# Two-layer image block: first strip's projection moved into the second unit of an image change, the mean of the second normalization later, the kept strip normalized after the copies of the weighted values

## The chip, the cores and the metric

The kernel runs on one core of one Trainium2 chip. The metric is the device time of one execution in microseconds. 3 runs of the kernel before took 3533.04 to 3534.71 us, with a median of 3534.49 us.

## The reference

The input x has 8 images of 384 channels and 64 x 64 pixels, all in float32. Two layers are added to it:

- Layer 1: group normalization (32 groups), then, per pixel, a layer normalization over the channels and a product with a 384 x 1152 matrix for queries, keys and values. Half of the channels go to attention in 8 x 8 windows (branch 0, 4 heads), the other half to attention in windows shifted by 4 pixels with wrap-around (branch 1, 4 heads, with a mask). Both have a position bias and a softmax. The joined result goes through the 384 x 384 output projection and is added to x.
- Layer 2: group normalization of the sum, a 384 x 384 product per pixel, in each 8 x 8 patch a Fourier transform, a filter and the transform back, a 3 x 3 depthwise convolution, a gelu of one half times the other half, and a 192 x 384 product, added to x.

```
x = x + attention(_gn(x))          # layer 1
x = x + fourier_conv(_gn(x))       # layer 2
```

The second group normalization needs mean and variance over the whole image. So layer 2 of an image cannot begin before layer 1 of that image has been projected for all of its strips.

## The kernel before, in words

**Strips and units.** An image is cut into 8 strips of 8 rows, 512 pixels each (NS = 8), with the channels in three groups (KC = 3) on 128 partitions. A strip's attention takes two units, one for each branch: strip s of image b has its units at 16 b + 2 s and one more. Layer 2 of image b runs through the same units as layer 1 of image b + 1: strip s starts at unit 16 b + 18 + 2 s. Units are counted from 0 in the text. An even unit holds four `mix` products (pt) and the end of an older strip (`finish`, pw), an odd one the transform back (`back`, pz) and usually a projection (pr). The image change of image b is units 16 b + 16 and 16 b + 17: both of the last projections of image b lie at it, those of strip 7 and of strip 0. Strip 0 comes so late because its first rows, by the wrap-around, come from strip 7's shifted windows. Its data lies in a buffer of its own (tag `ow`, one buffer). Unit 16 b + 17 has no projection in the kernel before and is the shortest.

**Order.** Every piece of work is put down with a place by `at(place, piece, ...)`. The list is sorted by place and issued in this order. Matmuls stay exactly in this order (`keep_in_program_order`). On the other engines, a scheduler takes, when an engine is free in its own account of time, the ready instruction that was issued first; the order is then fixed. Extra edges without a wait fix an order on one engine: `after_softmax` (behind the last softmax instruction issued) and `after_out` (behind the last copy of the weighted values, `zs["out"]`). Large transfers on SP wait for a gate, the last copy of the first qk tile (`in_dense_work`).

**Pieces that matter here**, for a unit w:

- `scores` (w + 0.05): 64 small matmuls into pS. `weights`, `exponent`, `divide` (0.12 to 0.26): softmax on DVE and ACT.
- `turn` (w + 0.80): transposes the weights into pT; ACT copies them to eT. `apply` (w + 1.00): 64 small matmuls of eT with v into pA. `put` (w + 1.07): ACT copies pA to o (L602 to L605 for branch 1), and ten or five transfers on POOL's queue write o to the projection's input oT.
- pS, pT, pA and one half of pw share two PSUM pairs (`psum2`); all other products share four PSUM banks (`psum`).
- `qk_tile`, `v_tile` (places 0.14 to 0.88 of the unit before): products pq and pvv with their copies on ACT.
- `project`: 9 matmuls pr of 512 columns for a strip, in three groups m, each followed on DVE by an addition into x_add. `keep`: bn_stats of the three parts. `store`: x_add to memory.
- `second_mean`: bn_aggr (mv_b), matmul pm, four small DVE instructions. `second_std`: matmul pv, square root on ACT (sd, with a table load), reciprocal and shift on DVE.
- `normal_x1`: three activations xn for a strip of layer 2. Strip 0's x_add stays in its buffer and is used again here (the load "mix" for s = 0 is only a renaming); the other strips come from memory (x_mix). xn has one buffer.
- `conv`: 24 multiply-adds ("taps", zz L785) a strip on DVE, most of DVE's work.

**Empty instructions.** `EMPTY` gives, unit by unit, a number of empty TensorE instructions that are issued among the dense matmuls of that unit (qk tiles and projections).

Of the kernel before, what the change touches and what calls it, by code (L numbers as in the profile page):

```python
# [8 lines left out]
AF = mybir.ActivationFunctionType  # L9
# [9 lines left out]
NS = SW // WS  # L19
# [6 lines left out]
C_ID, C_ONES, C_GRP, C_FWD, C_INV, C_MASK = 0, 128, 256, 384, 512, 640  # L26
C_PICK = C_MASK + 3 * 64
N_CONST = C_PICK + 2
EMPTY = (129, 0, 0, 96, 52, 0, 0, 98, 11, 124, 11, 124, 3, 124, 11, 124, 11, 45, 43, 124, 52, 123, 11, 124,
         11, 124, 11, 124, 3, 124, 11, 124, 11, 45, 43, 124, 52, 123, 11, 124, 11, 124, 11, 124, 3, 124, 11, 124,  # L30
         11, 45, 43, 124, 52, 123, 11, 124, 11, 124, 11, 124, 3, 124, 11, 124, 11, 45, 43, 124, 52, 123, 11, 124,
         11, 124, 11, 124, 3, 124, 11, 124, 11, 45, 43, 124, 52, 123, 11, 124, 11, 124, 11, 124, 3, 124, 11, 124,
         11, 45, 43, 124, 52, 123, 11, 124, 11, 124, 11, 124, 11, 0, 0, 115)

STATS_AT = 2.16, 4.16, 5.16, 6.16, 7.16, 8.16, 9.16, 10.16

# [2 lines left out]
def block_kernel(ctx: ExitStack, tc: tile.TileContext, out, x, consts, fsel, wqk, wv, bqk, bv,  # L39
                 wp, bp, lng, lnb, rpb1, rpb2, w_in, w_dw, w_out, filt):  # L40
    nc = tc.nc
    B = x.shape[0]
# [72 lines left out]
    for s in range(NS):  # L115
        tag, bufs = ("x", 5) if s < 5 else (("xn", 1), ("ow", 1), ("y2", 1))[s - 5]
        t = strip(tag, bufs, f"x_first{s}")
# [28 lines left out]
    for j, to, n, t, hp, of in blocks:  # L146
        nc.gpsimd.dma_start(out=bqk_sb[to:to + n].rearrange("p (b j) -> p b j", b=2)[:, :, j],
                            in_=bqk[of:of + n, 4 * t:4 * t + 4].rearrange("p (b i) -> p b i", b=2)[:, :, hp])
# [19 lines left out]
    for br, tab in ((0, rpb1), (1, rpb2)):  # L168
        raw = sb.tile([P, 2, 64], F32, tag="t2", bufs=3, name=f"rpb_raw{br}")
        raw_bias.append(raw)  # L170
        for h in range(4):
            half = slice(h % 2 * 64, h % 2 * 64 + 64)
            for y2 in range(WS):
                nc.gpsimd.dma_start(
                    out=raw[half, h // 2, y2 * WS:(y2 + 1) * WS],
                    in_=bass.AP(tab.tensor, h * 225 + y2 * 15, [[15, 8], [1, 8], [1, 8]]),
# [109 lines left out]
    def image_order(t):  # L286

        return t.rearrange("p (r w c) -> p w r c", r=WS, w=NS)

    def by_window(t):  # L290

        return t.rearrange("p (w r c) -> p w r c", w=NS, r=WS)
# [7 lines left out]
    def at(place, piece, *args):  # L300
        plan.append((place, len(plan), piece, args))

    xs, ys, y2s, qks, vs, os_, ots, x1s, zs = ({} for _ in range(9))
# [10 lines left out]
    gs0, gs1, st0s, st1s, x1d = ({} for _ in range(5))  # L314
# [9 lines left out]
    def in_dense_work(i):  # L324


        if zs.get("gate"):
            behind(i, zs["gate"], mybir.DependencyClass.Sync, "transfer in dense work")
# [4 lines left out]
    def load(b, s, what):  # L333

        if b == 0 and (what == "stats" or what == "norm" and s < 3):
            xs[b, s, what] = first_x[s]
            return
        if what == "mix" and s == 0:
            xs[b, s, what] = xs.pop((b, s, "add"))
            return  # L340
        t = xs[b, s, what] = strip("x", 5, f"x_{what}_{b}_{s}")
        src = x1d[b][s] if what in ("mix", "finish") else rows_of(x[b], s)
        in_dense_work(nc.sync.dma_start(out=t, in_=src))
# [239 lines left out]
    def after_out(i):  # L583
        if "out" in zs:
            behind(i, zs["out"], mybir.DependencyClass.NoSync, "weighted values first")
# [47 lines left out]
        strip_stats(st1s[b], s, xs[b, s, "add"])  # L633

    def store(b, s):
        in_dense_work(nc.sync.dma_start(out=x1d[b][s], in_=xs[b, s, "add"] if s == 0 else xs.pop((b, s, "add"))))


    def second_mean(b):
# [9 lines left out]
    def normal_x1(b, s):  # L649

        t, (gain, shift) = xs.pop((b, s, "mix")), gs1[b]
        xn = x1s[b, s] = strip("xn", 1, f"xn_{b}_{s}")
        for k in range(KC):
            nc.scalar.activation(by_window(xn[:, k, :]), image_order(t[:, k, :]), AF.Identity,  # L654
                                 bias=shift, scale=gain)

    def mix(b, s, i):

# [189 lines left out]
    for b in range(B):  # L848
        first = 2 * NS * b

        for s in range(NS):
            u = first - 16 + STATS_AT[s] if b else -10 + 0.1 * s
            at(u, load, b, s, "stats")
            at(u + (0.5 if b else 0.05), input_stats, b, s)
        if b == 0:

            at(-9.99, pack_qk, 0)
            at(-9.98, qk_weights, 0)
            at(-9.97, v_weights)
            at(-9.96, pack_qk, 1)  # L860
            at(-9.95, qk_weights, 1)
            for place, key in ((-9.82, ("qk", 0)), (-9.62, ("v",)), (-2.9, ("qk", 1))):
                at(place, take_off, *key)
            at(-2.64, qk_bias, 0)
            at(-2.58, v_bias)
            at(-2.58, qk_bias, 1)
            at(-2.7, spread_first)
            at(-0.6, position_bias, 0)
            at(-0.4, position_bias, 1)
            at(0.2, out_bias)  # L870
            at(0.2, filter_weights)
        at(first - 4.8 if b else -8, input_mean, b)
        at(first - 4.4 if b else -7.9, input_std, b)
        for s in range(NS):
            u = first + 2 * s

            v = u - 4
            early = 1.75 if b == 0 and s == 1 else 0
            at(v - 0.84 - early, load, b, s, "norm")
            at(v + 0.15 - early, group_normal, b, s)  # L880
            at(v + 0.45 - (1.35 if early else 0), ln_square, b, s)
            if b:
                at(v + 0.985, small_tiles, v + 1)
            at(v + 0.99 if (b, s) != (0, 1) else -2.69, ln_sums, b, s)
            at(v + 0.99 if (b, s) != (0, 1) else -2.6, ln_row, b, s)
            at(v + 1.35, ln_scale, b, s)

            if s:
                at(v + 1.50, shifted_half, b, s - 1, 1)
            else:  # L890
                at(u - 1.15, shifted_half, b, NS - 1, 1)
            at(u - 1.2 if s < NS - 1 else v + 1.55, shifted_half, b, s, 0)
            for br in range(2):
                w = u + br
                for t in range(3):
                    at(w - 1 + (0.14, 0.34, 0.55)[t], qk_tile, b, s, br, t)
                for g in range(2):
                    at(w - 1 + ((0.78, 0.86), (0.67, 0.88))[br][g], v_tile, b, s, br, g)
                at(w + 0.05, scores, b, s, br)
                at(w + 0.12, weights, b, s, br)  # L900

                at(w + 0.13, exponent, b, s, br)
                at(w + (0.23, 0.26)[br], divide, b, s, br)
                at(w + 0.80, turn, b, s, br)
                at(w + 1.00, apply, b, s, br)
                at(w + 1.07, put, b, s, br)

            if 0 < s < NS - 1:
                places = [u + 3 + f for f in (0.27, 0.45, 0.70)]
            else:  # L910
                places = [first + 2 * NS + f + (0.0 if s else 0.24) for f in (0.36, 0.44, 0.52)]
            at(int(places[0]) - 0.84, load, b, s, "add")
            for m in range(KC):
                at(places[m], project, b, s, m)
            at(places[2] + 0.1, keep, b, s)
            at(int(places[2]) + 1.15, store, b, s)
        first += 2 * NS
        at(first + 1.25, second_mean, b)
        at(first + (1.90 if b < B - 1 else 1.995), second_std, b)
        if b == B - 1:  # L920
            at(first + 2, tap_matrices)
        for s in range(NS):
            u = first + 2 + 2 * s
            at(u - 0.84, load, b, s, "mix")
            at(u + 0.02, normal_x1, b, s)
            for i in range(4):
                at(u + (0.28, 0.45, 0.60, 0.78)[i], mix, b, s, i)
            for j in range(2):
                at(u + (0.995, 1.02)[j], transform, b, s, j)
            if b < B - 1:  # L930
                at(u + 1.985, small_tiles, u + 2)
            at(u + 1.99, back, b, s)
            at(u + 2.08 if b < B - 1 or s < NS - 1 else u + 1.991, borders, b, s)

            for n, m in enumerate((0, 2, 1)):
                for tap in range(1, 6):
                    at(u + (2.62, 3.10, 3.5)[n] + 0.05 * tap + (0.4 if n == 2 and tap > 3 else 0), conv, b, s, m, tap)
                for tap in range(6, 9):
                    at(u + 4.2 + 0.25 * (n * 3 + tap - 6) / 9, conv, b, s, m, tap)
            if (b, s) in on_pool:  # L940
                for place, taps in ((2.45, (0, 1)), (2.8, (2, 3)), (3.15, (4, 5)), (4.15, (6, 7)), (4.3, (8,))):
                    at(u + place, pool_taps, b, s, taps)
            if (b, s) in on_pe:
                at(u + 2.3, conv_taps, b, s)
            at(u + 5.16, load, b, s, "finish")
            at(u + 4.5, gate, b, s)
            at(u + 6.10, finish, b, s)
# [5 lines left out]
    order = [p[2:] for p in sorted(plan, key=lambda p: p[:2])]  # L953
    dense, empty, counts = [], [0] * len(order), list(EMPTY)
    for i, (piece, args) in enumerate(order):
# [116 lines left out]
```

## Time and profile before

| | us |
|---|---|
| median of 3 runs | 3534.49 |
| profiled execution, device time | 3528.99 |
| its span, first to last instruction | 3526.8 |
| steady odd unit / even unit | 24.26 / 28.25 |
| units 48, 49, 50, 51, 52 (third image change) | 43.7, 18.15, 29.39, 17.69, 28.66 |

| engine | busy us | share |
|---|---|---|
| PE (TensorE matmuls) | 3450.3 | 98% |
| DVE | 3062.2 | 87% |
| ACT | 2535.8 | 72% |
| POOL | 1055.3 | 30% |

All times of instructions and units come from the one profiled execution. The mean granted TensorE clock is 0.992. In lines of the profile, `out<-in` are the program's names of tiles, Lnnn is a line of the kernel, and a bracket at the end of a timeline row is the idle time of the engine before the row and what ended it ("issue": nothing that the profile shows). Nearly all matmuls have line L62, that of a helper, so they are told apart by their tiles.

### The profile page before, as it was taken

The numbers are of one execution on the slowest core, as the hardware profiler recorded it, in microseconds if no ns is written. First come the engines' busy times: TensorE is split into PE (matmuls) and PEld (weight loads), VectorE is DVE, ScalarE is ACT, GpSimd is POOL, SyncE is SP. The second block draws the span as 40 slices with busy tenths as digits, with TensorE's granted clock in tenths as the row PEclk, the third lists the DMA queues.
The fourth block names the chain that finished last, engine by engine and source line by source line (L and its number), as shares of the span: only waits on it lengthen the run. The fifth ranks groups of instructions, "written<-read, shape, count | busy, mean of one in ns | idle before, by whom it ended". The sixth has DMA issues, their size and how long they took to land.

```text
span 3526.8 us, 93350 instructions
## 1 busy us (share of the span) xinstructions
PE 3450.3 (98%) x36454; PEld 2192.9 (62%) x36454; DVE 3062.2 (87%) x4330; ACT 2535.8 (72%) x4069; POOL 1055.3 (30%) x1688
## 2 busy tenths in 40 slices
PE   7999999999999999999999999999999999999888
PEld 5666666666666666666666666666666666666554
DVE  5676589889998899998999889998899988987987
ACT  5877777768777687776777767777777767776574
POOL 6433222323222232222233223232232223222244
PEclk8999999999999999999999999999999999999999
DMA  4343234323343334333344324433234333323432
GB/s 135 117 128 100 88 119 138 107 101 133 130 148 108 117 107 153 120 121 109 119 136 140 119 89 141 138 116 133 101 118 156 113 107 109 108 99 104 160 109 81
DMA packets 176101, 421.13 MB, mean 119 GB/s; under 512 B 26656, under 2 KB 29243, under 8 KB 175688
## 3 DMA queue, kind: packets, MB, share of 16 engines
q1 hardware_dynamic: 138832, 364.25, 29.6%
q0 software_dynamic: 36416, 50.65, 5.1%
q8 instruction: 316, 5.18, 0.6%
q14 instruction: 97, 0.79, 0.1%
q10 hardware_dynamic: 440, 0.27, 0.0%
HBM read 263.92 MB, written 100.79 MB: 103 GB/s over the span
## 4 chain that ended last, share of the span: by engine, by line
PE 87%; DVE 8%; ACT 2%; issue 1%; DMA 1%; POOL 0%; SPq 0%; ACTq 0%; POOLq 0%; DVEq 0%
PE pq L62 26%; PE pr L62 14%; PE pvv L62 13%; PE pt L62 11%; PE pw L62 6%; PE pA L62 3%; PE pz L62 3%; PE pT L70 3%; PE pS L62 3%; DVE zz L785 2%; PE pf L62 2%; DVE acc L785 1%; PE ln L62 1%; DVE t L681 1%; ACT tap L753 1%
## 5 line engine op out<-in xcount | busy, mean ns | idle before, releaser
L785 DVE SCALAR_TENSOR_TENSOR zz<-z,dw_sb,zz 128x512 f32<-128x512 f32 x1331 | 1026.5, 797 | 10.8
L62 PE MATMUL pq<-y,wqk_sb 128*128 128x512 f32 x2160 | 989.4, 597 | 0.9 <-ACT kcd L470 0.7
L615 POOL DMA_DIRECT2D oT<-o x960 | 480.2, 508 | 963.4 <-ACT z L718 431.2
L62 PEld LDWEIGHTS pq<-y,wqk_sb 128*128 128x128 f32 x2160 | 403.1, 190 | 448.0 <-issue 407.3
L62 PE MATMUL pt<-wi_sb,xn 128*128 128x384 f32 x1536 | 535.1, 487 | 3.0 <-ACT xn L654 3.0
L62 PE MATMUL pr<-oT,wp_sb 128*128 128x512 f32 x1152 | 523.9, 593 | 1.6 <-DMA oT<-o 1.6
L62 PE MATMUL pvv<-wv_sb,y 128*128 128x192 f32 x2880 | 507.4, 326 | 0.0
L62 PEld LDWEIGHTS pvv<-wv_sb,y 128*128 128x128 f32 x2880 | 471.7, 190 | 48.6 <-issue 33.7
L62 PEld LDWEIGHTS pt<-wi_sb,xn 128*128 128x128 f32 x1536 | 290.9, 191 | 232.8 <-issue 74.1
L452 POOL COPY y<-y 128x384 f32<-128x384 f32 x112 | 86.0, 768 | 1108.0 <-PE pvv L62 643.7
L62 PEld LDWEIGHTS pr<-oT,wp_sb 128*128 128x128 f32 x1152 | 217.5, 190 | 263.7 <-issue 246.3
L470 ACT ACTIVATE kcd<-pq,bqk_sb 32x512 f32<-32x512 f32 x512 | 348.4, 680 | 9.1
L470 ACT ACTIVATE qab<-pq,bq_sb,cst 96x512 f32<-96x512 f32 (+1 forms) x256 | 197.7, 772 | 181.1 <-PE pq L62 178.7
L503 ACT COPY v<-pvv 128x384 f32<-128x384 f32 x256 | 121.4, 474 | 191.5 <-PE pvv L62 190.0
L470 ACT ACTIVATE kab<-pq,bqk_sb 96x512 f32<-96x512 f32 (+1 forms) x256 | 174.1, 680 | 90.4 <-PE pq L62 86.1
L470 ACT ACTIVATE qcd<-pq,bq_sb,cst 96x512 f32<-96x512 f32 (+1 forms) x256 | 197.4, 771 | 33.5 <-PE pq L62 27.7
L382 POOL TENSOR_TENSOR sq<-sq 128x512 f32<-128x512 f32 x122 | 201.4, 1651 | 5.8
L537 DVE TENSOR_TENSOR e<-e,mx 128x1024 f32<-128x1024 f32 x128 | 199.3, 1557 | 3.9
L530 DVE TENSOR_TENSOR e<-pS,bias 128x512 f32<-128x512 f32 (+2 forms) x200 | 108.1, 547 | 93.9 <-PE pS L62 93.9
L547 DVE TENSOR_REDUCE rc<-e 128x16 f32<-128x1024 f32 x128 | 155.1, 1211 | 35.2 <-ACT e L542 35.1
L62 PE MATMUL pw<-zz,wo_sb 128*128 128x512 f32 x496 | 182.2, 509 | 0.0
L625 DVE SCALAR_TENSOR_TENSOR x_add<-pr,vec,x_add 128x512 f32<-128x512 f32 x192 | 142.6, 743 | 38.9 <-PE pr L62 38.2
(166 smaller groups left out, 5376.3 us busy)
## 6 DMA issues: line engine op xcount, KB each, us to landing
x_add<-in_x_dram SPq DMA_DIRECT2D x64, 768.0 KB
x1d<-x_add SPq DMA_DIRECT2D x64, 768.0 KB
x_finish<-x1d SPq DMA_DIRECT2D x64, 768.0 KB
out_dram<-x_finish SPq DMA_DIRECT2D x64, 768.0 KB
x_norm<-in_x_dram SPq DMA_DIRECT2D x61, 768.0 KB
x_stats<-in_x_dram SPq DMA_DIRECT2D x56, 768.0 KB
x_mix<-x1d SPq DMA_DIRECT2D x56, 768.0 KB
oT<-o POOLq DMA_DIRECT2D x192, 96.0 KB, 3.7
```

The source lines that it names most:

```text
L62: tc.keep_in_program_order(nc.tensor.matmul(*args, **kw))
L70: tc.keep_in_program_order(nc.tensor.transpose(*args, **kw))
L382: nc.gpsimd.tensor_tensor(sq[:, 0, :], sq[:, 0, :], sq[:, k, :], ALU.add)
L452: nc.gpsimd.tensor_copy(dst[:, :, :, :, 0:4], src[:, :, :, :, 4:8])
L470: return nc.scalar.activation(dst[to:to + n], pq[of:of + n], AF.Identity, bias=bias[of:of + n], scale=scale)
L503: nc.scalar.copy(v[:, 384 * g:384 * (g + 1)], pvv[:, 0:384])
L530: nc.vector.tensor_tensor(e5[:, odd, :, a:z, :], pS[:, odd, :, a:z, :], bias_t[br, kind, odd].unsqueeze(2).to_broadcast([P, 2, z - a, 64]) ...
L537: zs["soft"] = nc.vector.tensor_tensor(e, e, mx.unsqueeze(2).to_broadcast([P, 2 * NS, 64]), ALU.subtract)
L547: nc.vector.tensor_reduce(rc, e, AX.X, ALU.add)
L615: nc.gpsimd.dma_start(out=oT[to % P:to % P + z - a, to // P, rows], in_=o[row + a:row + z, h // 2, of:of + n])
L625: after_softmax(nc.vector.scalar_tensor_tensor(t[:, m, :], pr, bp_sb[:, m:m + 1], t[:, m, :], ALU.add, ALU.add))
L785: i = nc.vector.scalar_tensor_tensor(acc.rearrange("p (r c) -> p r c", c=SW), z[:, dy:dy + 8, dx:dx + SW], dw_sb[:, m, TAPS[tap]:TAPS[tap] ...
```

## The change

For every image b:

- The three groups of strip 0's projection move from places 16.60, 16.68, 16.76 (counted from the image's first unit) to 17.115, 17.12, 17.125, so from the first unit of the change to the second, right behind the scores. What hangs on these places moves with them: the load of its x (15.16 to 16.16), `keep` (16.86 to 17.225), `store` (17.15 to 18.15).
- `second_mean` moves from 17.25 to 17.69. `second_std` stays at 17.90 (17.995 for the last image).
- `normal_x1` of strip 0 moves from 18.02 to 18.12 and, but for the last image, its activations get the edge behind the last copy of the weighted values. The renaming for "mix" of strip 0 comes at 17.70, before the store, so that now the store drops the name.
- `turn` of branch 1 moves from 0.80 to 0.95 in all odd units from 19 on. It thereby comes behind the second v tile (0.86 or so) and, in the second unit of a change, behind `second_std`.
- `EMPTY` has other numbers: per image change 83, 6, 53 in place of 45, 43, 52, and small changes at the first change and at the end.

```diff
-EMPTY = (129, 0, 0, 96, 52, 0, 0, 98, 11, 124, 11, 124, 3, 124, 11, 124, 11, 45, 43, 124, 52, 123, 11, 124,
+EMPTY = (129, 0, 0, 98, 53, 0, 0, 100, 11, 124, 11, 124, 3, 124, 11, 124, 11, 83, 6, 124, 53, 123, 11, 124,
...
         if what == "mix" and s == 0:
-            xs[b, s, what] = xs.pop((b, s, "add"))
+            xs[b, s, what] = xs[b, s, "add"]
             return
...
     def store(b, s):
-        in_dense_work(nc.sync.dma_start(out=x1d[b][s], in_=xs[b, s, "add"] if s == 0 else xs.pop((b, s, "add"))))
+        in_dense_work(nc.sync.dma_start(out=x1d[b][s], in_=xs.pop((b, s, "add"))))
...
         for k in range(KC):
-            nc.scalar.activation(by_window(xn[:, k, :]), image_order(t[:, k, :]), AF.Identity,
-                                 bias=shift, scale=gain)
+            i = nc.scalar.activation(by_window(xn[:, k, :]), image_order(t[:, k, :]), AF.Identity,
+                                     bias=shift, scale=gain)
+            if s == 0 and b < B - 1:
+                after_out(i)
...
-                at(w + 0.80, turn, b, s, br)
+                at(w + (0.95 if br and w > 2 * NS + 1 else 0.80), turn, b, s, br)
...
             if 0 < s < NS - 1:
                 places = [u + 3 + f for f in (0.27, 0.45, 0.70)]
+            elif s:
+                places = [first + 2 * NS + f for f in (0.36, 0.44, 0.52)]
             else:
-                places = [first + 2 * NS + f + (0.0 if s else 0.24) for f in (0.36, 0.44, 0.52)]
+                places = [first + 2 * NS + f for f in (1.115, 1.12, 1.125)]
...
-        at(first + 1.25, second_mean, b)
+        at(first + 1.69, second_mean, b)
...
-            at(u - 0.84, load, b, s, "mix")
-            at(u + 0.02, normal_x1, b, s)
+            at(u - (0.84 if s else 0.3), load, b, s, "mix")
+            at(u + (0.02 if s else 0.12), normal_x1, b, s)
```

## The prediction

> **What bounds the kernel now.** I read the page, the waits of TensorE, the times of single units (a unit runs from one block of score matmuls pS to the next), then the timeline at an image change.
>
> ```profile
> PE 3450.3 (98%) x36454; PEld 2192.9 (62%) x36454; DVE 3062.2 (87%) x4330; ACT 2535.8 (72%) x4069; POOL 1055.3 (30%) x1688
> ```
>
> TensorE is busy 98% and, by the page's fourth part, carries 87% of the chain that ended last. The change takes no matmul away, so only TensorE's idle time can be won. Three of TensorE's waits (columns: us in total, times, longest):
>
> ```profile
> PE pw L62 <- ACT o L605: 10.7, 10, 1.8
> PE pT L70 <- DVE e L549: 4.6, 6, 1.1
> PE pA L62 <- issue: 4.1, 6, 1.0
> ```
>
> They sum to 19.4 us; what is idle besides lies in the start and in the tail behind all attention. Nearly all of the 19.4 is at image changes, as the windows by unit show (columns: length, then busy time and count of PE, PEld, DVE, ACT, POOL, clock, DMA):
>
> ```profile
> 1175.81:1219.52 43.71, 43.71 (x325) 25.10 (x320) 32.82 (x46) 22.52 (x40) 9.93 (x18) 1.00 0.13 46
> 1219.52:1237.67 18.15, 17.15 (x285) 12.60 (x277) 17.58 (x29) 16.07 (x24) 5.14 (x9) 1.00 0.62 211
> 1237.67:1267.06 29.39, 28.54 (x289) 18.18 (x285) 27.24 (x37) 24.44 (x41) 10.83 (x15) 1.00 0.21 69
> 1337.66:1365.91 28.25, 28.25 (x288) 18.26 (x284) 26.20 (x36) 21.97 (x39) 10.42 (x15) 1.00 0.40 128
> ```
>
> These are units 48 (where both projections of the change lie now), 49 (the short unit), 50, and a steady even unit, 54. Steady units have no idle TensorE. Units 49 and 50 take 47.54 together, where 17.15 + 28.25 = 45.40 would do: 2.14 us lost. Two more windows, the pair of units 33+34 and its five successors, and the pair 35+36 and its five:
>
> ```profile
> sum 285.23, PE 274.09 PEld 184.66 DVE 267.80 ACT 243.53 POOL 94.54; mean PE 45.68 PEld 30.78 DVE 44.63 ACT 40.59 POOL 15.76
> ```
> ```profile
> sum 278.01, PE 271.80 PEld 180.67 DVE 269.71 ACT 223.13 POOL 92.33; mean PE 45.30 PEld 30.11 DVE 44.95 ACT 37.19 POOL 15.39
> ```
>
> Each of the first six takes 47.53 to 47.54, although the gap before pA varies from 0.08 to 1.00 among them: something other than TensorE pins the pair. The timeline of ACT and PE shows it:
>
> ```profile
> 1234.08 1.28 ACT L283 ACT_TABLE_LOAD   x1
> 1235.38 0.26 ACT L283 ACTIVATE sd_b<-pv_b,eps_t 128x1 f32<-128x1 f32 x1
> 1235.54 1.18 ACT L709 ACTIVATE z<-pz 128x512 f32<-128x512 f32 x2
> 1236.72 2.23 ACT L654 ACTIVATE xn<-x_add,sh,gs_b 128x512 f32<-128x512 f32 x3
> 1238.85 0.64 ACT L709 ACTIVATE z<-pz 128x512 f32<-128x512 f32 x1
> 1239.37 0.56 ACT L602 COPY o<-pA 128x512 f32<-128x512 f32 x1
> ...
> 1240.30 0.23 ACT L605 COPY o<-pA 128x64 f32<-128x64 f32 x1
> ```
> ```profile
> 1237.03 0.85 PE L62 MATMUL pA<-eT,v 64*64 64x64 f32 x41 [1.00 <-issue]
> ...
> 1240.59 0.66 PE L62 MATMUL pw<-g,wo_sb 64*64 64x256 f32 x8 [0.85 <-ACT o L605]
> ```
>
> The second half of pw needs the PSUM pair that pA filled. ACT empties it (o, L602 to L605) only after it has normalized the kept strip (xn, 2.23 us).
>
> **The change part by part.**
>
> *xn behind the copies.* Take 2.23 us from in front of o. On the clock of unit 49 before, pA would end at 1237.9 (next paragraph); three z copies end at 1238.4, the o copies take 1.16 (1239.37 to 1240.53), so L605 ends near 1239.6. pS ends at 1238.8 and eight pw follow for 0.9: no wait. xn then follows the six border copies (0.9) and ends near 1242.7; the first pt needs it after pw and a qk tile, some 7 us after pw starts, near 1245.8. If that cover went, 2.2 us per change would return.
>
> *pA and the weights' transpose.* Turn moves from 0.80 to 0.95 in odd units, so pT comes after the second pvv and after pv_b, and eT after sd. In the short unit: the second v copy (the row before those shown) to 1234.07, table load to 1235.36, sd to 1235.64, eT 1.02 more: 1236.65. TensorE does pT (0.9) and pz (1.95) from 1233.6 and wants eT at 1236.35: 0.45 lost with 0.15 for the signal. The row has 1.28 for the load and sd 1.30 behind its start.
>
> [...]
>
> *Fetch gap.* The 1.00 before pA is no data wait. In unit 49 the DMA share is 0.62: two stores, x_finish and x_norm start at once there. One store leaves for unit 50 and the unit gets 3.9 us longer, so I take this gap as gone; since the pair was pinned by xn it is not counted twice. [...]
>
> So the pair keeps 0.45 and the 28.54 - 28.25 = 0.29 in unit 50: 0.74 instead of 2.14. Gain 1.40 x 6 = 8.4. The first change (units 17 and 18, 0.72 issue and 0.69 wait on kcd) gives 1.4 more.
>
> *Projection moved.* Nine pr at 0.43 (18 take 7.89) leave unit 48 for 49: 3.9 us each way, zero net. DVE follows with three x_add (0.66 apart) and three bn_stats (0.60): 3.8 us. DVE is 17.58 of 18.15 busy in unit 49, so it gets 21.4 of some 21.5: full.
>
> *Mean late.* pm goes from behind the first qk tile to behind the third: TensorE reaches it 1.1 + 3.9 + 7.9 = 12.9 us into the unit. Queued behind a waiting pm are both pvv, pT, pz, pA. mv (0.8) ends on DVE after: the transform's t until 1.8, softmax's first part 3.9, x_add 2.0, bn_stats 1.8, two taps 1.3 and the first reduce of divide 1.2: 12.8. Ends: 0, or, if all eight taps of lower place, ln_scale and the whole divide come first (5.6 + 1.7 + 2.7 instead of 2.5), 20.3 and so a wait of 7.4. I take 0: in unit 49 the mean's small instructions slip in between taps (1225.67, 1226.45, 1227.24).
>
> *Turn in the other odd units.* Steady: pT's end to eT's end 1.15, pz 1.95 covers it with 0.65 to spare. In the unit of strip 1 (51) pT waits 0.70 for the end of divide and ACT is late:
>
> ```profile
> 1280.70 0.81 ACT L654 ACTIVATE xn<-x_mix,sh,gs_b 128x512 f32<-128x512 f32 x1 [0.36 <-DMA x_mix<-x1d]
> ...
> 1281.42 0.99 ACT L559 COPY eT<-pT 128x1024 f32<-128x1024 f32 x1
> ```
>
> The 0.70 goes (5 times: 3.5), but eT now queues behind two or three xn and the second v: end 1283.6 to 1284.3, against pA's 1283.50 now. Between a gain of 3.5 + 2.0 (pw in unit 52 and its like) and a loss of 0.95 x 6 = 5.7 I take 0.
>
> *Free edits.* The x_add load one unit later has unit 48's 40 us to land. Strip 0's store in unit 50 waits for the same gate as x_stats, ahead of it on SP; DMA share there is 0.21. On POOL the issues of the new strip 0's oT (1222.22, five, 2.53) now wait for the last pr, some 2.2 us; behind them POOL's next is a memset at 1227.38. Two more empty instructions per change lie in dense work, where unit 54 is gapless. Were these covers gone: a few tenths each.
>
> *Tail.* At the last change the projection comes after pt and pf (3.4 us) and pm follows it: mv 2.4 after the last pr, so pm at 3323.3 against 3320.95; DVE took up pm only at 3322.87, so some 0.9 is lost, between -1 and 3. I take 1.0.
>
> Sum: 8.4 + 1.4 - 1.0 + 0 = 8.8 us. The profiled execution took 3529.0 (span 3526.8 and 2.2 around it): 3520.2. The median is 5.5 above that execution: 3525.7.
>
> **Rivals.** *Strip 1 gains too* (ACT has eT in time): another 5.5, 3520.2. For: unit 115 has no pT wait and no loss. Against: the xn rows above. *Strip 1 eats it*: eT behind three xn, 5.7, and sd's stall twice my size, 2.7: 0.4 gained, 3534. For: ACT has 15.60 of 17.68 us in unit 51. *The late mean becomes TensorE's bound* (slower): DVE is full in the short unit; every us that mv comes after 12.9 costs 6 us over the six changes that carry a transform. From 1.5 us on it eats the gain; mv behind the whole divide and two taps more (1.5 + 1.3) is about 3 us: 18 - 8.8, so 3543.7. For: 21.4 of 21.5 busy. Against: the mean's slips between taps.
>
> **How the numbers follow.** Forecast 0.50 (3521 to 3529 by itself), strip 1 gains 0.18, eaten 0.10, late mean 0.22. A measurement tells 0.2%, 7.1 us, from nothing: faster is below 3527.4. Four fifths of the forecast and all of the first rival lie there: 0.58. The rest of the forecast and the second rival: 0.20. Slower 0.22. The range 3518 to 3546 leaves out the best of the first rival and the late mean from 3.4 us on.
>
> **What would show it.** Right: pairs 33+34 near 45.40 + 3.87 + 0.74 = 50.0, xn after L605, no pw wait on L605, unit 48 near 39.9. Wrong: a pm wait on mv in the short unit, pA waiting on eT in odd units, or steady odd units above 24.26.

## The result and the profile after

The changed kernel is slower: 3540.48 us (median of 22 runs, 3533.87 to 3546.68) against 3532.21 us for the kernel before in the same sessions (22 runs, 3528.73 to 3541.57), a ratio of 1.0022 with a 95% interval of 1.0016 to 1.0028. The profiled execution after took 3535.11 us, with a span of 3533.0; that of before 3528.99 and 3526.8. So the two profiles show 6.2 us of the 8.3 between the medians.

In the page's first part the engines' loads are nearly as before:

```profile
PE 3451.4 (98%) x36454; PEld 2196.8 (62%) x36454; DVE 3051.5 (86%) x4330; ACT 2534.6 (72%) x4069; POOL 1054.4 (30%) x1688
```

Three of TensorE's waits (us in total, times, longest), which are others than before:

```profile
PE pm_b L62 <- DVE mv_b L267: 17.5, 7, 3.6
PE pA L62 <- ACT eT L559: 10.8, 7, 2.5
PE pw L62 <- ACT o L605: 1.3, 1, 1.3
```

At the image changes the three waits shown of before (pw on o, pT on e, pA on issue) are gone. In their place pm waits for the mean and pA for the copy eT. Six of pm's seven waits lie at the image changes; the seventh, of 3.56 us, lies in the tail, behind the last image's strips. pA's seven lie in strip 1's second units. The windows of units 49 to 51, and the sums over the pairs 33+34 and 35+36 with their five successors (columns as before: length, busy time of PE, PEld, DVE, ACT, POOL, clock, DMA):

```profile
1210.57:1239.64 29.07, 26.76 (x303) 17.44 (x296) 23.86 (x39) 15.06 (x23) 5.14 (x9) 0.94 0.32 105
1239.64:1267.86 28.22, 28.22 (x289) 18.12 (x283) 25.25 (x33) 25.20 (x43) 10.80 (x15) 1.00 0.29 99
1267.86:1287.11 19.25, 16.80 (x282) 12.10 (x274) 18.53 (x27) 16.09 (x25) 4.99 (x8) 1.00 0.48 159
```
```profile
sum 337.50, PE 323.61 PEld 207.09 DVE 293.62 ACT 242.05 POOL 94.38; mean PE 53.93 PEld 34.51 DVE 48.94 ACT 40.34 POOL 15.73
```
```profile
sum 280.25, PE 270.07 PEld 181.35 DVE 269.51 ACT 223.38 POOL 92.14; mean PE 45.01 PEld 30.23 DVE 44.92 ACT 37.23 POOL 15.36
```

Unit 50 has no idle TensorE any more. All the loss of the first pair now lies in the short unit, and strip 1's second unit (51) has 2.45 us idle. Because the projection moved from unit 32 to unit 33, the first pair is best read together with unit 32. Units 32 to 34 and their five successors take 547.54 us before and 553.47 after; with no idle TensorE at the full clock they take 534.71 (an experiment below reached that). So the change took away all of the 12.8 us that stood there before, and put 18.8 in their place: six waits of pm of 2.31 us (13.9), 0.28 more beside each (1.7), and 3.2 from a halved clock, below. Units 35+36 and successors got 2.2 longer, the first change (units 16 to 19) 1.1 shorter, the tail 0.6 shorter.

Why pm waits is seen on DVE in unit 33, which starts at 784.93:

```profile
795.33 0.69 DVE L260 BATCH_NORM_STATS2 st<-x_add 128x6 f32<-128x512 f32 x1
...
796.58 1.22 DVE L549 TENSOR_TENSOR e<-e,rc 128x1024 f32<-128x1024 f32 x1
797.72 0.74 DVE L787 SCALAR_TENSOR_TENSOR zz<-z,dw_sb,zz 128x512 f32<-128x512 f32 x1
798.38 1.75 DVE L438 TENSOR_TENSOR y<-y,rs 128x1536 f32<-128x1536 f32 x1
800.05 3.18 DVE L787 SCALAR_TENSOR_TENSOR zz<-z,dw_sb,zz 128x512 f32<-128x512 f32 x4
803.15 0.79 DVE L267 BATCH_NORM_AGGREGATE mv_b<-st 128x2 f32<-128x144 f32 x1
```
```profile
804.00 0.38 PE L62 MATMUL pm_b<-mv_b,cst 128*128 128x1 f32 x2 [2.31 <-DVE mv_b L267]
```

The last statistics are done at 796.0. TensorE arrives at pm at 801.69, 5.7 us later. The mean isn't late for its data: it is issued at 17.69, and in DVE's fixed order the end of divide, ln_scale and six taps of lower stand between.

In strip 1's second unit ACT has xn ahead of eT:

```profile
1282.58 1.52 ACT L654 ACTIVATE xn<-x_mix,sh,gs_b 128x512 f32<-128x512 f32 x2 [1.47 <-DMA x_mix<-x1d]
...
1285.08 0.99 ACT L559 COPY eT<-pT 128x1024 f32<-128x1024 f32 x1
```
```profile
1286.13 1.16 PE L62 MATMUL pA<-eT,v 64*64 64x64 f32 x64 [2.45 <-ACT eT L559]
```

Unit 49 is 1.6 us longer than unit 33, whose wait is the same. Short windows behind the pm of unit 49 (at 1229.64) show the clock:

```profile
1229.60:1231.00 1.40, 1.36 (x5) 1.36 (x6) 1.32 (x4) 0.28 (x1) 0.00 (x0) 0.50 1.03 391
1231.00:1233.00 2.00, 2.00 (x8) 2.00 (x7) 1.32 (x6) 0.00 (x0) 0.00 (x0) 0.52 0.18 60
1233.00:1235.50 2.50, 2.50 (x18) 2.50 (x18) 1.91 (x4) 0.48 (x1) 0.00 (x0) 1.00 0.00 0
```

TensorE works, but at half clock for 3.41 us. This happened in two of the six changes (units 49 and 97), and nowhere between units 1 and 126 before.

### The profile page after: what moved, and what is told of

Its sections match the earlier page's. It is cut to its first block, busy times and chain, and to the rows that moved or that the text cites. A ratio compares the mean times of both kernels' runs of the same rounds, so it can differ in the third digit from the quotient of the medians.

```text
span 3533.0 us, 93336 instructions
## 1 busy us (share of the span) xinstructions
PE 3451.4 (98%) x36454; PEld 2196.8 (62%) x36454; DVE 3051.5 (86%) x4330; ACT 2534.6 (72%) x4069; POOL 1054.4 (30%) x1688
## 5 line engine op out<-in xcount | busy, mean ns | idle before, releaser
L542 ACT ACTIVATE e<-e 128x1024 f32<-128x1024 f32 x128 | 135.3, 1057 | 58.5 <-DVE e L537 56.8
```

What stands on the lines that cost most here:

```text
L542: nc.scalar.activation(e, e, AF.Exp)
```

## The experiments

Theory: the late mean and strip 1's late eT make the loss; xn behind the copies is a gain. Rival: the projection in the short unit, or the late turn in that unit, is what costs. The kernel before was run beside each (medians 3531.2 to 3531.8). "Units 32 to 34" and "35+36" are sums over six changes in the profiled execution; "halved" counts stretches at half clock in units 33 to 116 (one in run 2 and the one in run 5 last 6.83 us, all others 3.41).

| kernel | median us (range, runs) | ratio, 95% interval | units 32 to 34 | 35+36 | halved |
|---|---|---|---|---|---|
| before | 3532.21 (3528.73 to 3541.57, 22) | 1 | 547.54 | 278.01 | 0 |
| after | 3540.48 (3533.87 to 3546.68, 22) | 1.0022, 1.0016 to 1.0028 | 553.47 | 280.25 | 2 |
| 1 after, early bn_aggr | 3517.68 (3515.78 to 3520.55, 5) | 0.9961, 0.9948 to 0.9975 | 534.71 | 279.75 | 1 |
| 2 after, strip 1's turn early | 3537.08 (3533.23 to 3545.11, 11) | 1.0015, 1.0006 to 1.0024 | 560.02 | 278.08 | 5 |
| 3 before, strip 0's xn late | 3520.24 (3518.10 to 3525.60, 5) | 0.9967, 0.9955 to 0.9980 | 538.85 | 277.00 | 0 |
| 4 before, turn late | 3544.84 (3537.78 to 3546.22, 7) | 1.0031, 1.0021 to 1.0042 | 562.63 | 273.69 | 6 |
| 5 = 3 + 4 | 3523.97 (3517.49 to 3533.22, 11) | 0.9980, 0.9971 to 0.9989 | 535.07 | 284.58 | 1 |
| 6 = 1 + 2 | 3512.90 (3509.76 to 3517.96, 5) | 0.9949, 0.9937 to 0.9962 | 534.70 | 278.29 | 0 |
| 7 = 1 + strip 1's xn late | 3507.03 (3501.67 to 3511.69, 5) | 0.9931, 0.9918 to 0.9945 | 534.71 | 268.71 | 0 |
| 8 = 7, all turns early | 3507.11 (3505.21 to 3512.01, 5) | 0.9935, 0.9922 to 0.9947 | 534.33 | 274.78 | 0 |
| 9 after, strip 1's xn late | 3521.85 (3519.82 to 3531.81, 10) | 0.9975, 0.9966 to 0.9984 | 551.91 | 268.70 | 1 |
| 10 = 7, bn_aggr at 1.57 | 3516.61 (3514.14 to 3520.47, 5) | 0.9958, 0.9945 to 0.9972 | 547.92 | 268.70 | 1 |
| 11 before, xn of strips 0, 1 late | 3514.22 (3510.30 to 3517.57, 5) | 0.9952, 0.9939 to 0.9964 | 537.18 | 273.45 | 0 |
| 12 = 11 + turn late | 3509.57 (3509.01 to 3515.51, 5) | 0.9943, 0.9931 to 0.9956 | 536.44 | 268.70 | 0 |

**1. The mean's bn_aggr early, everything else as after.** second_mean is split; its first instruction is issued at 17.23, the rest stays at 17.69.

```diff
+        at(first + 1.23, second_aggr, b)      # mv = bn_aggr(st1s)
         at(first + 1.69, second_mean, b)      # matmul pm and the rest
```

> The kernel after, with bn_aggr of the second mean issued at 17.23 instead of 17.69 (counted from the image's first unit); the matmul pm stays at 17.69. Theory (order on DVE): pm waited 2.31 us because bn_aggr stood behind divide's end, ln_scale and six taps; it now stands behind the third bn_stats and one tap. The pm wait goes in all six changes (13.9 us of the profiled execution), and with it the two stretches of half TensorE clock behind it (1.6 us each): the short unit falls from 27.5 and 29.1 to about 25.2, and the kernel lies 15 to 18 us under after, 8 to 11 under before. Rival (DVE is simply full in the short unit): what moves up pushes the rest back; TensorE then waits as long at pT or at the next unit's scores and softmax, and the kernel stays within 4 us of after.

Measured 3517.68, 22.8 us under after's median from other sessions, more than was expected. Profile against profile it is 17.8 us under after. pm waits no more at the six changes, and the pairs 33+34 are without any idle TensorE:

```profile
sum 318.77, PE 318.77 PEld 204.15 DVE 291.47 ACT 242.32 POOL 94.72; mean PE 53.13 PEld 34.02 DVE 48.58 ACT 40.39 POOL 15.79
```

So the projection in the short unit and the turn behind sd cost nothing there. The loss of after in these units is the place of one DVE instruction of 0.8 us.

**2. Turn at 0.80 again in strip 1's second unit alone** (units 19, 35, 51, ...).

```diff
-                at(w + (0.95 if br and w > 2 * NS + 1 else 0.80), turn, b, s, br)
+                at(w + (0.95 if br and w > 2 * NS + 1 and w % (2 * NS) != 3 else 0.80), turn, b, s, br)
```

> The kernel after, with turn back at 0.80 in strip 1's second unit (unit 35 and its five successors, and unit 19) and at 0.95 elsewhere. Theory (three xn in front of eT on ACT): with the old place ACT's order is v, xn, eT, xn, v, xn again; the pA wait on eT (1.6 to 2.5 us, 0.6 in the last) goes and the pT wait on divide of 0.7 comes back; units 35 and the like fall from 18.4 to 19.3 to about 17.4, in all 5 to 8 us under after. Rival (the late landing of x_mix is what holds eT, in either order): the first xn still stands in front of eT, so pA still waits about 1 us and less than 3 us are won. The pm wait of 2.31 stays in both.

The sum of 35+36 falls by 2.2 us, with pT waiting on divide (0.7 at five changes) and pw on o (0.4 to 0.9 at six) where pA waited on eT. But the profiled execution hides it: behind pm the clock was halved in five changes, in one of them (unit 49) for two windows of 3.41 us, six windows in place of two, and units 32 to 34 are 6.5 longer at the same pm wait of 2.31. The median is 3.4 under after; with ranges as wide as these it says little by itself.

**3. Before, with only strip 0's xn behind the copies** (place 18.12 and the edge behind the copies, as in the change).

```diff
+            if s == 0 and b < B - 1:
+                after_out(i)
...
-            at(u + 0.02, normal_x1, b, s)
+            at(u + (0.02 if s else 0.12), normal_x1, b, s)
```

> The kernel before, with only the kept strip's three activations put behind the copies of the weighted values (place 18.12 and the edge), nothing else. Theory (xn pins the pair of units 33+34 at 47.54): the pw wait on L605 goes; what is left of the pair is the fetch gap before pA (up to 1.0) and 0.3: 45.7 to 46.7, so 5 to 10 us under before. Rival (the chain through the second normalization or the fetch pins the pair, xn only fills it): the pair stays within 0.3 us of 47.54 and the kernel within 2 us of before.

Measured 3520.24, 11.6 under before, a little more than the theory's 5 to 10. Units 32 to 34 gain 8.7; the pair 33+34 takes 46.1 on the mean, as the theory had it. The profiled execution (3525.6) is the slowest of the five, with a tail of 256.9 us where the other kernels have 250 to 254; I read nothing from it. pA's wait on issue, 4.1 before, is still there with 5.4 in total.

**4. Before, with only the late turn.**

```diff
-                at(w + 0.80, turn, b, s, br)
+                at(w + (0.95 if br and w > 2 * NS + 1 else 0.80), turn, b, s, br)
```

> The kernel before, with only turn of branch 1 at 0.95 in the odd units from 19 on. Theory: steady odd units stay at 24.26; in strip 1's unit the pT wait of 0.7 turns into a pA wait on eT of 1.5 to 2.5 us; units 35+36 and their successors lose 0.3 to 1.0 us each, 2 to 6 us over before. First forecast's working: between 5.5 us under and 5.7 over, 0 taken. Rival (the late turn is free or wins its 0.7): 3 us or more under before.

Slower by 13 us, far beyond what I expected. Strip 1 gains 4.3. In the first pair eT, and so pA, come later; o stands on ACT behind xn and z as before, and the second half of pw waits for it longer. Behind the wait the clock is halved, six times of six:

```profile
1245.59 1.02 PE L62 MATMUL pw<-g,wo_sb 64*64 64x256 f32 x8 [2.44 <-ACT o L605]
1246.54 4.14 PE L62 MATMUL pw<-zz,wo_sb 128*128 128x512 f32 x8
```
```profile
1245.76:1249.17 3.41, 3.41 (x11) 1.20 (x8) 0.52 (x1) 2.63 (x7) 3.35 (x7) 0.50 0.23 63
```

Unit 50 takes 32.87 us, of which 2.44 are the wait; its TensorE is busy 30.43 instead of the 28.2 of an undisturbed one (1.7 of it from the clock, as behind pm in after). So, by this estimate, the clock makes some 10 (6 x 1.7) of the 15.1 us by which units 32 to 34 are longer.

**5. Before, with both.**

> The kernel before with two edits: the kept strip's xn behind the o copies, and the late turn (0.95) in odd units; projection and mean stay where they were. Theory A (the late turn cost 13 us by itself only because xn pinned the pair and the wait it made was long enough to halve TensorE's clock six times): with xn away, units 33+34 are 17.19 + 28.21 plus at most 0.5, units 35+36 45.6, no half clock in units 33 to 116, and the time is 3513 to 3518, some 3 to 6 under the xn edit alone (3520.2). Rival B (the late turn costs by eT coming behind sd and xn, whatever stands behind): 3526 to 3534, the 13 us added to the xn edit.

3523.97: the 13 us of the late turn are not added, so rival B falls; but it is above the range of theory A. The first pair is as A had it (535.07, near the floor of 534.71); the miss is strip 1, 284.58, with pA waiting up to 2.9 us on eT. In run 4, with the same turn, it was 273.69. In run 4 xn of unit 51 did not wait for its data; here it waited 1.86 us for x_mix, at the head of ACT's queue, and eT behind it (first row: run 4, unit from 1273.70; second: this run, unit from 1267.52):

```profile
1286.57 1.52 ACT L654 ACTIVATE xn<-x_mix,sh,gs_b 128x512 f32<-128x512 f32 x2
```
```profile
1282.67 1.52 ACT L654 ACTIVATE xn<-x_mix,sh,gs_b 128x512 f32<-128x512 f32 x2 [1.86 <-DMA x_mix<-x1d]
```

Both issue x_mix 5.9 us into the unit, between two other transfers of 768 KB. Why it landed later here I did not settle.

**6. After, with early bn_aggr and strip 1's turn at 0.80.**

> The kernel after with the mean's bn_aggr issued early (as in the run that took the pm wait away) and turn back at 0.80 in strip 1's second unit alone. Theory A (in strip 1 the late turn is paid as pA's wait on eT, the early one as pT's wait on divide, and the late one loses by 0.4 us per change; the half clock seen behind the pm wait goes with the pm wait): units 33, 49, ... 24.91, units 35+36 near 46.3, no half clock there, 3514 to 3517 against 3517.7 with the early bn_aggr alone. Rival B (turn in strip 1 is worth nothing either way, or helps): 3517 to 3521.

3512.90, 4.8 under run 1 and a little better than theory A's range; no halved stretch is left between units 1 and 126. By the sums, though, strip 1's turn is worth nothing by itself (rival B): units 35+36 are 1.5 shorter, and all of that is the one halved stretch of run 1 (unit 36 takes 29.85, behind a pA wait of 2.27). Another 0.9 is in unit 19. The rest of the 4.8 I can't place.

**7. After, with early bn_aggr and strip 1's xn also behind the copies.**

```diff
-            if s == 0 and b < B - 1:
+            if s < 2 and b < B - 1:
                 after_out(i)
...
-            at(u + (0.02 if s else 0.12), normal_x1, b, s)
+            at(u + (0.12 if s < 2 else 0.02), normal_x1, b, s)
```

> The kernel after with the mean's bn_aggr issued early and strip 1's xn also behind the last put copy of the unit before. Theory A (pA waits on eT in strip 1's second unit because the xn copies that wait for x_mix stand ahead of it on ScalarE): pA's wait there falls to 0.9 or less, units 35+36 fall from 46.6 to 45.6 on the mean, 3510 to 3514. Rival B (eT is late there for divide and the two v copies, not for xn): pA's waits stay at 0.9 to 2.3 and the time at 3516 to 3519; with xn so late that the next pt waits, up to 3530.

3507.03: the best version, 24.6 us under before in the same session. pA waits no more in any odd unit, and the pairs 35+36 have no idle TensorE:

```profile
sum 268.71, PE 268.71 PEld 181.36 DVE 263.54 ACT 225.03 POOL 94.25; mean PE 44.78 PEld 30.23 DVE 43.92 ACT 37.50 POOL 15.71
```

pA waited for xn, then, not for divide or v.

**8. The same, with turn at 0.80 everywhere.**

> The same, with turn back at 0.80 in all odd units. If the late turn is worth something once xn is out of its way: pT waits on divide in strip 1's second unit (0.7 to 1.1), pw on o in the unit behind, and the time is 2 to 6 over the kernel with the late turn. If the late turn is worth nothing: within 1.5 of it. If it costs (eT behind sd and its table load, 0.3 to 0.5 per change): 2 to 4 under it.

The median is the same (3507.11). The profile has units 35+36 6.1 us longer, with pT waiting on divide 0.7 at five changes, as the first case said; its execution (3511.51) is also one of the two slowest of five. The five runs spread over 6.8 us, so the late turn's worth isn't settled by these two; runs 11 and 12 show it better.

**9. After, with strip 1's xn behind the copies as the only edit.** The late mean is kept.

> The kernel after with strip 1's xn behind the copies as the only edit: the late mean is kept. Theory A (the late mean costs 2.31 us of pm wait at each of six image changes, and on top 1.7 us for each change at which the clock is halved behind it; a change is halved when 2.04 us or more of the wait fall into one window of the 3.413 us grid, which the traces show): pm waits 2.31 six times, units 35+36 44.8, time 3507.0 + 13.9 = 3521 with no halving, 3531 with six; median 3521 to 3529 and runs spread over 6 us or more. Rival B (the cost of the change is strip 1's pA wait): 3507 to 3512.

3521.85, 14.8 above run 7. Where the change's late mean stays, its cost stays: 27.50 us in five of six short units, 24.91 in run 7. Nine of ten runs lie between 3519.8 and 3524.5 and one at 3531.8, about where theory A puts none to two halved changes, and six. Only the profiled run shows its halvings (one); that the slow run had six is not shown, though its mean granted clock is the lowest of the ten (0.990 against 0.991 to 0.993).

**10. Dose: bn_aggr one tap earlier than in after** (place 1.57 in run 7's kernel).

> The best kernel so far (early bn_aggr, strip 1's xn behind the copies) with bn_aggr put at 1.57 instead of 1.23, one tap of lower earlier on VectorE than in the kernel after: a pm wait of 2.31 - 0.79 = 1.5 us at six changes. Theory A (each us of wait costs six, and a wait of 1.5 can't fill 2.04 us of a window of the clock): 3507.0 + 9.1 = 3516, between 3514 and 3518, no stretch at 0.5 in units 33 to 116, runs no more than 6 us apart. Rival B (any pm wait halves the clock behind it): 3519 to 3526. Rival C (the wait is covered elsewhere): 3507 to 3511.

The wait is 1.65, and each short unit 26.83 to 26.84 but for one:

```profile
802.53 0.38 PE L62 MATMUL pm_b<-mv_b,cst 128*128 128x1 f32 x2 [1.65 <-DVE mv_b L643]
```

3516.61, 9.6 above run 7, for six waits of 1.65 plus 0.27 (11.5 by the units). A us of wait at each of the six changes costs about six us. But unit 33 was halved behind a wait of 1.65, which theory A had excluded: the limit of 2.04 us is not sharp.

**11 and 12. Before, with xn of strips 0 and 1 behind the copies, without and with the late turn.**

> The kernel before with the xn of strips 0 and 1 behind the copies, nothing else: projection, mean and turn as before. Theory A (moving the projection is worth nothing at the changes, and the late turn too; all the gain is in the two xn): 33+34 as with strip 0's xn alone (46.1 on the mean), 35+36 45.7, 3515 to 3519. Rival B (the projection's place is worth something to units 33+34, which have 45.4 in the best kernel and 46.1 here): nearer 3520 than 3515. Rival C (strip 1's xn does nothing without the late turn): 3520.

> The same with the late turn (0.95). Theory A (moving the projection is worth nothing at the changes): units 33+34 45.4 and 35+36 44.78 as in the best kernel, the tail 253.6 against 250 to 251 there, so 3507 to 3511. Rival B (the projection in the short unit shortens it by covering something): 3512 to 3517. Rival C (the late turn costs as it did with strip 0's xn alone): 3519 to 3522.

3514.22 and 3509.57. The first is slightly below theory A's range, the second in it. Without moving the projection at all, the kernel of run 12 comes within 2.5 us of the best, and the intervals overlap: moving the projection, with the other numbers of empty instructions and pm's later place that the two kernels also differ in, is worth the first change (1.4 us by the profiles) and at most 1.7 us in units 32 to 34, of which 1.6 is one gap in unit 49. With xn out of the way the late turn gains: 4.7 us by the medians, 5.5 by these two sums.

## Why the prediction was wrong

**xn behind the copies** was right: forecast 1.40 x 6 = 8.4, measured 8.7 alone (run 3). That the two numbers lie so close is in part luck: run 3 keeps gaps before pA of 0.6 to 1.3 us in four of the six short units, which the forecast took as gone, and has no late turn, for which the forecast took off 0.45 a change. In run 1, which has the moved projection and the late turn, all of the 2.14 a change is gone (12.8). The first o copies come 1.9 us ahead of xn (812.85 and 814.76 in unit 33), and unit 50 takes 28.21.

**eT behind sd in the short unit** was forecast to lose 0.45 a change and lost nothing: run 1 is gapless there. In unit 33 after, pA starts as pz ends, at 811.44:

```profile
808.92 1.28 ACT L283 ACT_TABLE_LOAD   x1
810.22 0.26 ACT L283 ACTIVATE sd_b<-pv_b,eps_t 128x1 f32<-128x1 f32 x1
810.38 1.00 ACT L559 COPY eT<-pT 128x1024 f32<-128x1024 f32 x1
```

The term had too little cover and too long a signal: pT and pz take 3.07 us on TensorE here (from 808.37), some 0.3 more than taken, and pA starts 0.06 us behind eT's end, not 0.15. sd starts 1.30 us behind the start of the table load (808.92 to 810.22), as in the row of before (1234.08 to 1235.38) that the forecast took it from.

**The fetch gap** was taken as gone and is gone: after and run 1 have no pA wait on issue among their larger waits, while run 3, with the projection where it was, still has 5.4 us of it. The prediction called the gap one of fetching without showing it. The traces bear it out: in all fourteen, the 57 waits of TensorE on issue between 81 and 3270 us end 1.25 to 1.61 us after the end of a transfer of 16 KB on queue q8 (instruction), of which there is one in some 11 us. No run moved the fetch alone, and why the gap goes with the projection's place is not shown. The edits taken as free cost nothing to be seen: runs 1 and 7 have gapless pairs.

**The projection moved** was zero net as said (unit 48: 43.7 to 35.98, and 24.91 in run 1's short unit), but its size was wrong: "nine pr" are 18 rows of the trace, 7.72 us and not 3.9. TensorE reached pm 16.8 us into the unit, not 12.9. With that, DVE is not full either: run 1's short unit has 22.57 us of DVE work in 24.91.

**The mean late, "I take 0"**, is the step that failed. mv ended 19.0 us into the unit, near the upper end of my own bound (20.3), not at 12.8. I had taken the mean's small instructions between taps as a sign that bn_aggr too would slip in; but DVE's order goes by place, and 17.69 puts it behind the end of divide, ln_scale and six more taps. The error in the projection hid part of it: with TensorE at 12.9 the wait would have been 6.1 and not 2.31. The term was 0; it measured 2.59 x 6 = 15.5 in both after and run 9. The rival that I gave 0.22, the late mean as TensorE's bound, is what happened; its price, 3 us a change and 3543.7, stands 3 us above the median, in part by luck: it had neither the clock's 3.2 us nor strip 1's 2.2, and a gain that was 5 us too small.

**The turn in strip 1's unit, "I take 0"**, lost 2.2 us. Both ends of my bound had a mechanism: the loss (eT behind xn) in after, the gain in runs 7 and 12, 9.3 us in the sum of 35+36 once xn stands behind the copies there too. Which end came was decided by xn: run 4 gained 4.3 with xn ahead of eT but its data there, after lost where xn waited for x_mix, and behind the copies xn no longer stands in the way.

**The clock** was in no term. Two halvings in the profile cost 3.2 us; none to six of them would, by this estimate, spread the runs over 10 us, of the 13 that after's range has. Only one run has a profile, but the mean granted clock goes the same way: 0.990 to 0.992 in the five shortest of the 22 runs, 0.988 to 0.990 in the five longest.

**The tail**, forecast to lose 1.0, shows 0.6 less, although pm waits 3.56 us there and not 0.9; between profiles of these kernels the tail varies by several us, so its length says nothing.

Of the signs that I had named for right, xn behind L605 and no pw wait on L605 at the changes came. Of those for wrong, two came, pm's wait on mv and pA's on eT; steady odd units kept their 24.25. In sum, the forecast had 8.8 us to gain. The removed part was larger (12.8 and 1.1), and 18.8 (3.2 of it by the clock) and 2.2 came back through two ordered queues, DVE's and ACT's.

## What to carry to other kernels

When a small instruction feeds a matmul that heads an ordered TensorE queue, cost it by its place in its own engine's order, row by row, and not by when its data are ready: here 0.8 us of bn_aggr, moved ahead of work that could come 0.8 us later without a wait, was worth 18 us in the profile. When one piece is moved out of a waiting engine's way, move its twins too: strip 1's xn was worth 10.7 us by the medians in the kernel after (run 7 against 1) and 6.0 in the kernel before (run 11 against 3), strip 0's 11.6 (run 3). Count a moved step's matmuls from the rows of the trace, since both ends of a race move with an error in it.

## What the runs showed of the hardware

In the clock records of the two traces before and after, the stretches at half clock (10 and 12, most of them in the start and the tail) begin, in each trace, within 0.01 us of one grid of 3.413 us, and last 3.41 us or a multiple, but for the last one, which ends with the record. The windows below are those of this grid. Over the fourteen traces, between unit 1 and unit 127: of the windows with 2.04 us or more without a matmul, all 14 were followed by a window at 0.50; of the eleven with 1.65 to 2.01 us, three; below that, none, but for two windows that were themselves at half clock, with 0.27 us (run 2, unit 49) and 0.94 us (run 5, unit 35) without a matmul: the clock stayed at 0.50 for a second window there, which no run explains. In after, pm waits 2.31 us at each of the six changes, and what differs is how much falls into one window: 2.18 and 2.32 us without a matmul, halved; 1.16, 1.46, 1.81 and 1.92, not. Each of the two windows at half clock cost 1.6 to 1.7 us (units 49+50 and 97+98 have TensorE busy for 54.98 and 55.07 us, the other four pairs for 53.38 to 53.40). In run 4 the changes lie 426.62 us apart, within 0.05 us of 125 times 3.4133, so one phase served all six; after, they lie 425.6 to 428.0 us apart, and the phase moves.
